# A selective state space recurrence: one state at a time over 128 channels, or 16 states of 8 channels in partitions

## The chip, the cores and the metric

The kernel runs on one core of one Trainium2 chip. The metric is the device time of one execution in microseconds (us). The engines are TensorE (PE in the profile; PEld is its weight load), VectorE (DVE), ScalarE (ACT), GpSimd (POOL) and SyncE (SP, which here only issues DMAs). All arithmetic of the changed part is in fp32.

## The reference

The program is a small two-layer model on x of shape 64 x 32 x 256 (64 sequences of 32 steps). It adds six terms to x one after the other: cross-attention, an RWKV block, a mixture of experts (layer 0), cross-attention with quantised weights, a state space block, a mixture of experts (layer 1). Only the state space block is changed. Cut to what matters, with 512 inner channels d and 16 states n:

```python
xz = x @ in_proj_w.T + in_proj_b
x_main, z = jnp.split(xz, 2, axis=-1)
xc = silu(conv(x_main))                    # 4 taps along the sequence
ssm = xc @ x_proj_w.T + x_proj_b
B_param, C_param = ssm[..., :16], ssm[..., 16:32]
delta = softplus(ssm[..., -1:])            # one step width per token
A = -jnp.exp(A_log)                        # (512, 16)

def step(h, ts):
    dt, B_t, C_t, x_t = ts
    dA = jnp.exp(A[None] * dt[:, :, None])
    dBx = dt[:, :, None] * B_t[:, None, :] * x_t[:, :, None]
    h = dA * h + dBx                       # (batch, 512, 16)
    y = jnp.einsum('bdn,bn->bd', h, C_t) + D * x_t
    return (h, y)

y = scan(step) * silu(z)
out = layernorm(y @ out_proj_w.T + out_proj_b + x)
```

Every pair of channel and state has a recurrence of its own along the sequence, and the output of a channel is a sum over its 16 states.

## The kernel before

The 2048 tokens are cut into four blocks of 512 tokens (`BT` = 512, 16 sequences of 32 steps). Stages 0 to 3 hold layer 0 and the second cross-attention, stage 4 the state space block, stage 5 the experts of layer 1. `layers()` writes down which stage of which block comes when; a scheduler then orders each engine's instructions by that order as a priority and puts the semaphores in. From block 0 on, stage 4 of a block stands ahead of the attention (`s3`) of a later block and the experts (`s5`) of the block before, so that they run side by side. Each engine then works strictly through its own list, and so does the DMA queue of SP.

Stage 4 has three parts. `ahead(b)` normalises x, projects it (L965), convolves it along the sequence and applies silu, which gives `xc` with 128 channels in partitions and 4 groups of channels c; a matmul gives B and C (`ssm`, 32 rows of 512 tokens), which go to DRAM as `rows`; another gives the step width `dt` on all partitions. `gates(v)` computes silu(z) as `zs`. `recur(b, v)` is the recurrence.

In `recur`, POOL first multiplies x by the step (`dtx`, L1036), ACT multiplies x by D (L1041), and then a loop runs over the 16 states n. For a state, its rows of B and C are read from DRAM and spread over all 128 partitions as `bc` (L1045, 512 KB each, on SP). For each of two pairs of channel groups (`c2`), POOL multiplies `dtx` by B into `g` (L1048, 1024 elements for each partition); then for each of the two groups ACT computes exp(A dt) into `h` in PSUM (L1052), DVE runs the scan along the sequence in place (L1053; `dt` of each sequence's first step is set to 1e20, so that nothing carries over), and DVE multiplies by C into `hc` (L1054). POOL adds `hc` to y (L1055). After the loop POOL multiplies y by the gate (L1058), PE projects it (`outps`, L1065), and the layer norm follows. `g`, `hc` and `bc` have two buffers each, `h` has two PSUM banks.

The PSUM banks are held by pools: `ps` (two banks, tag s) serves attention, `psh` (two) the `h` and `outps`, `psp` (one) the projections of `ahead` and `gates`, `psu` (one) the experts' `up`, `psacc` (two) the experts' sums.

Of the kernel before, what the change touches and what calls it, by code (L numbers as in the profile page):

```python
# [8 lines left out]
F32 = mybir.dt.float32  # L9
# [6 lines left out]
P = 128  # L16
# [54 lines left out]
def _chan(k, name, j=0):  # L71
    at = CHAN_AT[name] + j
    return k.chan[:, at : at + 1]
# [844 lines left out]
def _stage4(k, w, wk):  # L918

    nc, i = k.nc, k.i
    N, C = 16, 4
    win = _load_w(k, w, "L1_attn_in_projT", 2, 4 * D)
# [11 lines left out]
    beta = w.tile([P, D], F32, name="beta4", tag="beta4")  # L937
    nc.scalar.dma_start(gamma, i["L1_attn_ln_gamma"].partition_broadcast(P))
    nc.scalar.dma_start(beta, i["L1_attn_ln_beta"].partition_broadcast(P))
    A = w.tile([P, C, N], F32, name="A", tag="A")  # L940
    nc.scalar.dma_start(A, i["L1_attn_A_log"].rearrange("(c p) n -> p c n", p=P))
    nc.scalar.activation(A, A, AF.Exp)

    nc.vector.tensor_scalar(A, A, -1.0, -1e-18, ALU.mult, ALU.min)
# [8 lines left out]
    def ph(shape, name):  # L953
        return k.psh.tile(shape, F32, name=name, tag="h")

    def pp(shape, name):
        return k.psp.tile(shape, F32, name=name, tag="p")

    def tmp(shape, name):
        return wk.tile(shape, F32, name=name, tag="t4", bufs=3)  # L960
# [7 lines left out]
    def ahead(b):  # L968
        v = Ctx()

        xs = [k.x[b][:, j, :] for j in range(4)]
        v.mv, v.rstd = _stats(k, xs, "4")
        x2 = [tmp([P, 2, D], "xn4") for _ in range(2)]
        xn = [x2[j // 2][:, j % 2, :] for j in range(4)]
        for j in range(4):
            _norm(k, xn[j], xs[j], v.mv, v.rstd, j)
        v.xT = wk.tile([P, 2, BT], F32, name="xT4", tag="xT4", bufs=1)
        _to_channels(k, xn, lambda c, ps: nc.scalar.copy(v.xT[:, c, :], ps), pp)

        xc = wk.tile([P, C, 16, T], F32, name="xc", tag="xc")  # L980
        for c in range(C):
            xpad = xpads[c % 2]
            nc.scalar.activation(
                xpad[:, :, 3:], project(v, c, pp).rearrange("p (b t) -> p b t", t=T), AF.Identity, bias=_chan(k, "L1_attn_in_proj_b", c)
            )
# [12 lines left out]
        ssm_ps = pp([2 * N, BT], "ssm_ps")  # L998
        for c in range(C):
            nc.tensor.matmul(ssm_ps, wx[:, c, 0 : 2 * N], v.y[:, c, :], start=c == 0, stop=c == C - 1)  # L1000
        ssm = tmp([2 * N, BT], "ssm")
        nc.scalar.activation(ssm, ssm_ps, AF.Identity, bias=bx)
        v.rows = k.dram.tile([2 * N, BT], F32, name="rows", tag="rows", bufs=2)
        nc.sync.dma_start(v.rows, ssm)

        dt_ps = pp([P, BT], "dt_ps")
        for c in range(C):
            nc.tensor.matmul(dt_ps, wdt[:, c, :], v.y[:, c, :], start=c == 0, stop=c == C - 1)
# [12 lines left out]
        nc.vector.tensor_tensor(l_, l_, e_, ALU.subtract)  # L1021
        nc.vector.scalar_tensor_tensor(dt, dt, 0.0, l_, ALU.max, ALU.add)

        return v

    def gates(v):

        v.zs = wk.tile([P, C, BT], F32, name="zs", tag="zs", bufs=1)
        for c in range(C):
            nc.scalar.activation(v.zs[:, c, :], project(v, C + c, pp), AF.Silu, bias=_chan(k, "L1_attn_in_proj_b", C + c))  # L1030

    def recur(b, v):
        xs = [k.x[b][:, j, :] for j in range(4)]
        dt, y = v.dt, v.y
        dtx = wk.tile([P, C, BT], F32, name="dtx", tag="dtx", bufs=1)
        nc.gpsimd.tensor_tensor(dtx, y, dt.unsqueeze(1).to_broadcast([P, C, BT]), ALU.mult)  # L1036

        nc.gpsimd.memset(dt.rearrange("p (b t) -> p b t", t=T)[:, :, 0:1], 1e20)

        for c in range(C):  # L1040
            nc.scalar.activation(y[:, c, :], y[:, c, :], AF.Copy, scale=_chan(k, "L1_attn_D", c))  # L1041
        bc_rows = v.rows.rearrange("(two n) t -> n two t", two=2)
        for n in range(N):
            bc = wk.tile([P, 2, BT], F32, name="bc", tag="bc", bufs=2)
            nc.sync.dma_start(bc, bc_rows[n].partition_broadcast(P))  # L1045
            for c2 in range(0, C, 2):
                g = wk.tile([P, 2, BT], F32, name="g", tag="g", bufs=2)
                nc.gpsimd.tensor_tensor(g, dtx[:, c2 : c2 + 2], bc[:, 0:1, :].to_broadcast([P, 2, BT]), ALU.mult)  # L1048
                hc = wk.tile([P, 2, BT], F32, name="hc", tag="hc", bufs=2)
                for c in range(2):  # L1050
                    h = ph([P, BT], "h")
                    nc.scalar.activation(h, dt, AF.Exp, scale=A[:, c2 + c, n : n + 1])  # L1052
                    nc.vector.tensor_tensor_scan(h, h, g[:, c, :], 0.0, ALU.mult, ALU.add)  # L1053
                    nc.vector.tensor_tensor(hc[:, c, :], h, bc[:, 1, :], ALU.mult)  # L1054
                nc.gpsimd.tensor_tensor(y[:, c2 : c2 + 2], y[:, c2 : c2 + 2], hc, ALU.add)  # L1055
# [218 lines left out]
def _layouts(inputs):  # L1274
# [22 lines left out]
    for n in ("L1_xattn_ln_gamma", "L1_xattn_ln_beta", "L1_attn_ln_gamma", "L1_attn_ln_beta", "L1_attn_A_log"):  # L1297
        o[n] = a[n]
    for n in ("in_proj", "x_proj", "out_proj"):
        o[f"L1_attn_{n}T"] = a[f"L1_attn_{n}_w"].T  # L1300
    o["L1_attn_x_proj_b"] = a["L1_attn_x_proj_b"][:, None]
# [27 lines left out]
```

## Time and profile before

| | us |
|---|---|
| runs | 2099.62, 2093.59, 2099.14 (median 2099.14) |
| the profiled execution | 2096.84 |
| its span in the profile | 2095.1 |
| first and last start of the scan (L1053) in it | 785.6 and 1909.3 |

The mean granted clock of TensorE over the span is 0.836 of full speed. Times within the span are counted from its start. The profile gives for each engine the busy time and number of instructions; for a group of instructions (line, engine, operation, output and inputs, shapes, count) it gives the busy time, the mean of one in ns, and behind a second bar the idle time of the engine just before them with what ended it. "PE x512" counts matmul records.

| queue | packets | MB | share of the 16 engines |
|---|---|---|---|
| q1 (issued by SP) | 84868 | 147.69 | 23.0% |

### The profile page before, as it was taken

The numbers are of one execution on the slowest core, as the hardware profiler recorded it, in microseconds if no ns is written. First come the engines' busy times: TensorE is split into PE (matmuls) and PEld (weight loads), VectorE is DVE, ScalarE is ACT, GpSimd is POOL, SyncE is SP. The second block draws the span as 40 slices with busy tenths as digits, with TensorE's granted clock in tenths as the row PEclk, the third lists the DMA queues.
The fourth block names the chain that finished last, engine by engine and source line by source line (L and its number), as shares of the span: only waits on it lengthen the run. The fifth ranks groups of instructions, "written<-read, shape, count | busy, mean of one in ns | idle before, by whom it ended". The sixth has DMA issues, their size and how long they took to land. (4 is left out here: it accounts for less than half of the span.)

```text
span 2095.1 us, 20245 instructions
## 1 busy us (share of the span) xinstructions
PE 1644.2 (78%) x6455; PEld 834.1 (40%) x6455; DVE 1391.0 (66%) x2444; ACT 952.6 (45%) x2009; POOL 1013.9 (48%) x1037
## 2 busy tenths in 40 slices
PE   4778966669979788656487798887888987787798
PEld 2334534335545434433234344433444433233343
DVE  5587584775584559889767988655888755876100
ACT  3445342304434174444146566356557445664232
POOL 4445445312121325667625777513767634998000
PEclk8677977889989898558687899888799887999799
DMA  7654232210001011121011232112232112332021
GB/s 239 219 182 144 91 120 80 79 34 21 21 21 43 17 42 51 30 61 61 0 50 53 80 91 90 31 41 65 71 88 73 49 31 66 89 111 77 30 81 40
DMA packets 87540, 149.93 MB, mean 72 GB/s; under 512 B 7672, under 2 KB 51978, under 8 KB 85386
## 3 DMA queue, kind: packets, MB, share of 16 engines
q1 hardware_dynamic: 84868, 147.69, 23.0%
q10 hardware_dynamic: 2566, 0.96, 0.2%
q8 instruction: 51, 0.84, 0.2%
q14 instruction: 55, 0.45, 0.1%
HBM read 137.71 MB, written 10.91 MB: 71 GB/s over the span
## 5 line engine op out<-in xcount | busy, mean ns | idle before, releaser
L1048 POOL TENSOR_TENSOR g<-dtx,bc 128x1024 f32<-128x1024 f32 x128 | 300.4, 2353 | 194.8 <-DVE h L1053 89.4
L1053 DVE TENSOR_TENSOR_SCAN h<-h,g 128x512 f32<-128x512 f32 x256 | 307.3, 1218 | 49.9 <-ACT h L1052 35.1
L1160 PE MATMUL up<-xT,w 128*128 128x512 f32 x512 | 288.1, 678 | 42.5 <-ACT hid L1162 37.3
L1055 POOL TENSOR_TENSOR xc<-xc,hc 128x1024 f32<-128x1024 f32 x128 | 301.0, 2356 | 26.5 <-DVE hc L1054 14.8
L1168 PE MATMUL acc<-hid,w 128*128 128x512 f32 x512 | 250.9, 610 | 15.8 <-ACT hid L1164 15.7
L1052 ACT ACTIVATE h<-dt,A 128x512 f32<-128x512 f32 x256 | 174.0, 692 | 184.5 <-DVE hc L1054 183.3
L1054 DVE TENSOR_TENSOR hc<-h,bc 128x512 f32<-128x512 f32 x256 | 169.7, 679 | 2.9 <-POOL xc L1055 0.5
L1160 PEld LDWEIGHTS up<-xT,w 128*128 128x128 f32 x512 | 97.3, 209 | 165.3 <-issue 79.2
L839 ACT ACTIVATE p<-sc,nm 128x256 f32<-128x256 f32 x256 | 117.6, 471 | 94.5 <-DVE nm L835 83.2
L1162 ACT ACTIVATE hid<-up,chan 128x512 f32<-128x512 f32 x128 | 87.2, 681 | 159.5 <-PE up L1160 159.4
L614 PE MATMUL weps<-we,xT 128*128 128x512 f32 x256 | 139.3, 665 | 17.2 <-DVE x L616 13.9
L1168 PEld LDWEIGHTS acc<-hid,w 128*128 128x128 f32 x512 | 94.1, 194 | 128.2 <-issue 96.3
L828 PE MATMUL sc<-kT,qm 32*128 32x256 f32 x512 | 131.6, 448 | 14.9 <-DVE od L867 11.5
L852 PE MATMUL pt_ps<-ident,p 128*128 128x128 f32 x512 | 97.0, 328 | 53.7 <-ACT p L839 26.6
L833 DVE TENSOR_REDUCE nm<-sc 128x2 f32<-128x512 f32 x128 | 86.3, 686 | 56.2 <-PE sc L828 55.1
L89 POOL TENSOR_TENSOR rs_t<-rs_r 128x4 f32<-128x4 f32 (+3 forms) x138 | 29.7, 218 | 183.1 <-DVE rs_r L87 157.0
L852 PEld LDWEIGHTS pt_ps<-ident,p 128*128 128x128 f32 x512 | 69.5, 165 | 107.1 <-ACT p L839 64.4
L828 PEld LDWEIGHTS sc<-kT,qm 32*128 32x128 f32 x512 | 81.5, 208 | 70.5 <-DVE od L867 20.7
L230 POOL TENSOR_TENSOR cT<-cT,scb 128x2056 f32<-128x2056 f32 x16 | 74.5, 4657 | 53.5 <-DMA scb<-scales 51.8
L1181 DVE SCALAR_TENSOR_TENSOR o<-rT,gt,x 128x256 f32<-128x256 f32 x16 | 7.7, 483 | 139.4 <-PE rT L1180 132.5
L854 ACT COPY pt<-pt_ps 128x512 f32<-128x512 f32 x128 | 74.0, 588 | 40.5 <-PE pt_ps L852 40.3
L514 POOL TENSOR_TENSOR kk<-kk 128x512 f32<-128x512 f32 x32 | 33.1, 1040 | 103.8 <-ACT kk L513 103.8
(389 smaller groups left out, 3218.7 us busy)
## 6 DMA issues: line engine op xcount, KB each, us to landing
bc<-rows SPq DMA_DIRECT2D x64, 512.0 KB
w<-in_L_ffn_w_dram SPq DMA_DIRECT2D x64, 512.0 KB
cT<-in_ctxT_dram SPq DMA_DIRECT2D x16, 1028.0 KB
cq<-cq SPq DMA_DIRECT2D x32, 514.0 KB
cn<-in_ctx_dram SPq DMA_DIRECT2D x64, 256.0 KB
scb<-scales SPq DMA_DIRECT2D x16, 514.0 KB
kb<-steps SPq DMA_DIRECT2D x16, 514.0 KB
x<-in_x_dram SPq DMA_DIRECT2D x4, 512.0 KB
```

Source lines behind the costliest of these rows:

```text
L614: nc.tensor.matmul(ps, xT[:, c, r], we[:, c, e : e + 2, :], start=c == 0, stop=c == 1)
L828: nc.tensor.matmul(sc[h][:, f, :], qm[r, e + f].rearrange("p l n g -> p (l n g)"), kTs[e][r, f, :], start=True, stop=True,)
L839: nc.scalar.activation(w_[:, f, h - h0, :], sc[h][:, f, :], AF.Exp, bias=nm[:, e + f, h : h + 1], accum_out=sm[:, e + f, h : h + 1],)
L852: nc.tensor.transpose(pt_ps[:, h, m, :], ws[e0, hp][:, f, h, m * P : (m + 1) * P], k.ident)
L1048: nc.gpsimd.tensor_tensor(g, dtx[:, c2 : c2 + 2], bc[:, 0:1, :].to_broadcast([P, 2, BT]), ALU.mult)
L1052: nc.scalar.activation(h, dt, AF.Exp, scale=A[:, c2 + c, n : n + 1])
L1053: nc.vector.tensor_tensor_scan(h, h, g[:, c, :], 0.0, ALU.mult, ALU.add)
L1054: nc.vector.tensor_tensor(hc[:, c, :], h, bc[:, 1, :], ALU.mult)
L1055: nc.gpsimd.tensor_tensor(y[:, c2 : c2 + 2], y[:, c2 : c2 + 2], hc, ALU.add)
L1160: nc.tensor.matmul(u, w1[e][:, c, q * P : (q + 1) * P], xT[:, c, :], start=c == 0, stop=c == 1)
L1162: nc.scalar.activation(hid[e][:, q, :], u, AF.Identity, bias=b1)
L1168: nc.tensor.matmul(acc[o], w2[e][:, q, o * P : (o + 1) * P], hid[e][:, q, :], start=n == H, stop=n == E * H + H - 1)
```

## The change

The recurrence is laid out the other way round. A tile of 128 partitions holds 16 states of 8 channels. The 512 channels are 64 such tiles, so the loop still has 64 scans of 128 x 512 for a block.

- `A` is laid out on the host as 16 states times 8 channels in partitions and 64 columns.
- B and C of a block are read from DRAM once, into `bc`, with each state's row spread over its 8 partitions (two DMAs of 256 KB).
- x times the step is computed in `ahead`, per channel group, and written to DRAM as `dtx` (four DMAs of 256 KB). For each pass of the loop two DMAs on SP read 8 channels each from there, spread over the 16 states, into the two halves of `g` (256 KB each); POOL multiplies `g` by B in place.
- The sum over the states is made by TensorE: a matmul with a 0/1 matrix (`red`, a window of 32 columns) adds the 16 states of 8 channels and puts them into their rows of a PSUM bank `y_ps`; 16 matmuls of 128 x 32 by 128 x 512 fill the 128 channels of a group. The sums of a pass are issued after the work of the next pass (`late`). One DVE operation for each group then adds D times x (in place of the multiplication on ACT), and POOL multiplies by the gate.
- POOL's additions of `hc` into y are gone. `g` and `hc` have three buffers in place of two.
- The projections of `ahead` take their PSUM from `ps` (the attention's), those of `gates` from `psu` (the experts'), and `psp` holds `y_ps`.

The diff, cut to its core:

```diff
-    A = w.tile([P, C, N], F32, name="A", tag="A")
-    nc.scalar.dma_start(A, i["L1_attn_A_log"].rearrange("(c p) n -> p c n", p=P))
+    G = 16
+    A = w.tile([P, C * G], F32, name="A", tag="A")
+    nc.scalar.dma_start(A, i["L1_attn_A_log"])
+
+    red = w.tile([P, 56], F32, name="red", tag="red")
+    nc.gpsimd.memset(red, 0.0)
+    nc.vector.tensor_reduce(red[:, 24:32], k.ident.rearrange("p (n d) -> p d n", d=8), AX.X, ALU.add)
...
-    def pp(shape, name):
-        return k.psp.tile(shape, F32, name=name, tag="p")
+    def pa(shape, name):
+        return k.ps.tile(shape, F32, name=name, tag="s")
+
+    def pz(shape, name):
+        return k.psu.tile(shape, F32, name=name, tag="u")
...
-        v.rows = k.dram.tile([2 * N, BT], F32, name="rows", tag="rows", bufs=2)
-        nc.sync.dma_start(v.rows, ssm)
+        rows = k.dram.tile([2, N, BT], F32, name="rows", tag="rows", bufs=2)
+        nc.sync.dma_start(rows.rearrange("w n t -> (w n) t"), ssm)
+        v.bc = wk.tile([P, 2, BT], F32, name="bc", tag="bc")
+        for j in range(2):
+            nc.sync.dma_start(v.bc[:, j], rows[j].unsqueeze(1).to_broadcast([N, 8, BT]))
...
+        v.dtx = k.dram.tile([2 * C, 8 * G // 2, BT], F32, name="dtx", tag="dtx", bufs=2)
+        for c in range(C):
+            dtx = tmp([P, BT], "dtx")
+            nc.gpsimd.tensor_tensor(dtx, v.y[:, c], dt, ALU.mult)
+            nc.sync.dma_start(v.dtx[2 * c : 2 * c + 2].rearrange("h p t -> (h p) t"), dtx)
+
+        nc.gpsimd.memset(dt.rearrange("p (b t) -> p b t", t=T)[:, :, 0:1], 1e20)
...
-        dtx = wk.tile([P, C, BT], F32, name="dtx", tag="dtx", bufs=1)
-        nc.gpsimd.tensor_tensor(dtx, y, dt.unsqueeze(1).to_broadcast([P, C, BT]), ALU.mult)
-
-        nc.gpsimd.memset(dt.rearrange("p (b t) -> p b t", t=T)[:, :, 0:1], 1e20)
-
+
+        dtx = v.dtx.rearrange("h (r q d) t -> h q r d t", r=2, d=8)
+
+        def total(c, q, h2, hc, ps):
+            for r in range(2):
+                m = 32 * (2 * h2 + r)
+                nc.tensor.matmul(
+                    ps[m : m + 32, :], red[:, 24 - 8 * q : 56 - 8 * q], hc[:, r, :], start=q == 0, stop=q == 3, skip_group_check=True,
+                )
+            if q == 3 and h2 == 1:
+                nc.vector.scalar_tensor_tensor(y[:, c, :], y[:, c, :], _chan(k, "L1_attn_D", c), ps, ALU.mult, ALU.add)
+                nc.gpsimd.tensor_tensor(y[:, c, :], y[:, c, :], v.zs[:, c, :], ALU.mult)
+
+        late = []
         for c in range(C):
-            nc.scalar.activation(y[:, c, :], y[:, c, :], AF.Copy, scale=_chan(k, "L1_attn_D", c))
-        bc_rows = v.rows.rearrange("(two n) t -> n two t", two=2)
-        for n in range(N):
-            bc = wk.tile([P, 2, BT], F32, name="bc", tag="bc", bufs=2)
-            nc.sync.dma_start(bc, bc_rows[n].partition_broadcast(P))
-            for c2 in range(0, C, 2):
-                g = wk.tile([P, 2, BT], F32, name="g", tag="g", bufs=2)
-                nc.gpsimd.tensor_tensor(g, dtx[:, c2 : c2 + 2], bc[:, 0:1, :].to_broadcast([P, 2, BT]), ALU.mult)
-                hc = wk.tile([P, 2, BT], F32, name="hc", tag="hc", bufs=2)
-                for c in range(2):
-                    h = ph([P, BT], "h")
-                    nc.scalar.activation(h, dt, AF.Exp, scale=A[:, c2 + c, n : n + 1])
-                    nc.vector.tensor_tensor_scan(h, h, g[:, c, :], 0.0, ALU.mult, ALU.add)
-                    nc.vector.tensor_tensor(hc[:, c, :], h, bc[:, 1, :], ALU.mult)
-                nc.gpsimd.tensor_tensor(y[:, c2 : c2 + 2], y[:, c2 : c2 + 2], hc, ALU.add)
-
-        for c2 in range(0, C, 2):
-            nc.gpsimd.tensor_tensor(y[:, c2 : c2 + 2], y[:, c2 : c2 + 2], v.zs[:, c2 : c2 + 2], ALU.mult)
-        xn = wk.tile([P, 4, D], F32, name="xe4", tag="hc", bufs=2)
+            ps = k.psp.tile([P, BT], F32, name="y_ps", tag="p")
+            for n in range(8):
+                q, h2 = divmod(n, 2)
+                g = wk.tile([P, 2, BT], F32, name="g", tag="g", bufs=3)
+                for r in range(2):
+                    nc.sync.dma_start(g[:, r], dtx[2 * c + h2, q, r].unsqueeze(0).to_broadcast([N, 8, BT]))
+                nc.gpsimd.tensor_tensor(g, g, v.bc[:, 0:1, :].to_broadcast([P, 2, BT]), ALU.mult)
+                hc = wk.tile([P, 2, BT], F32, name="hc", tag="hc", bufs=3)
+                for r in range(2):
+                    h = ph([P, BT], "h")
+                    at = c * G + 4 * (2 * h2 + r) + q
+                    nc.scalar.activation(h, dt, AF.Exp, scale=A[:, at : at + 1])
+                    nc.vector.tensor_tensor_scan(h, h, g[:, r, :], 0.0, ALU.mult, ALU.add)
+                    nc.vector.tensor_tensor(hc[:, r, :], h, v.bc[:, 1, :], ALU.mult)
+                late.append((c, q, h2, hc, ps))
+                if len(late) > 1:
+                    total(*late.pop(0))
+        total(*late.pop(0))
+
+        xn = wk.tile([P, 4, D], F32, name="xe4", tag="hc", bufs=3)
```

More of the change, by code (lines that the diff above doesn't have):

```diff
@@ L977, in ahead @@
         v.xT = wk.tile([P, 2, BT], F32, name="xT4", tag="xT4", bufs=1)
-        _to_channels(k, xn, lambda c, ps: nc.scalar.copy(v.xT[:, c, :], ps), pp)
+        _to_channels(k, xn, lambda c, ps: nc.scalar.copy(v.xT[:, c, :], ps), pa)
         xc = wk.tile([P, C, 16, T], F32, name="xc", tag="xc")
@@ L983, in ahead @@
             nc.scalar.activation(
-                xpad[:, :, 3:], project(v, c, pp).rearrange("p (b t) -> p b t", t=T), AF.Identity, bias=_chan(k, "L1_attn_in_proj_b", c)
+                xpad[:, :, 3:], project(v, c, pa).rearrange("p (b t) -> p b t", t=T), AF.Identity, bias=_chan(k, "L1_attn_in_proj_b", c)
             )
@@ L995, in ahead @@
         v.y = xc.rearrange("p c b t -> p c (b t)")
-        ssm_ps = pp([2 * N, BT], "ssm_ps")
+        ssm_ps = pa([2 * N, BT], "ssm_ps")
         for c in range(C):
@@ L1002, in ahead @@
         nc.scalar.activation(ssm, ssm_ps, AF.Identity, bias=bx)
-        v.rows = k.dram.tile([2 * N, BT], F32, name="rows", tag="rows", bufs=2)
-        nc.sync.dma_start(v.rows, ssm)
-        dt_ps = pp([P, BT], "dt_ps")
+        rows = k.dram.tile([2, N, BT], F32, name="rows", tag="rows", bufs=2)
[3 more added lines that the diff above has]
+            nc.sync.dma_start(v.bc[:, j], rows[j].unsqueeze(1).to_broadcast([N, 8, BT]))
+        dt_ps = pa([P, BT], "dt_ps")
         for c in range(C):
@@ L1029, in gates @@
         for c in range(C):
-            nc.scalar.activation(v.zs[:, c, :], project(v, C + c, pp), AF.Silu, bias=_chan(k, "L1_attn_in_proj_b", C + c))
+            nc.scalar.activation(v.zs[:, c, :], project(v, C + c, pz), AF.Silu, bias=_chan(k, "L1_attn_in_proj_b", C + c))
     def recur(b, v):
@@ L1296, in _layouts @@
     o["L1_xattn_woT"] = a["L1_xattn_wo"].T
-    for n in ("L1_xattn_ln_gamma", "L1_xattn_ln_beta", "L1_attn_ln_gamma", "L1_attn_ln_beta", "L1_attn_A_log"):
+    for n in ("L1_xattn_ln_gamma", "L1_xattn_ln_beta", "L1_attn_ln_gamma", "L1_attn_ln_beta"):
         o[n] = a[n]
+    o["L1_attn_A_log"] = a["L1_attn_A_log"].reshape(64, 8, 16).transpose(2, 1, 0).reshape(P, 64)
     for n in ("in_proj", "x_proj", "out_proj"):
```

## The prediction

> **What bounds the kernel now.** I read the page first (engine shares, costliest groups), then the table of stages, then the waits of the stages in which the recurrence runs, then single instructions.
>
> ```profile
> PE 1644.2 (78%) x6455; PEld 834.1 (40%) x6455; DVE 1391.0 (66%) x2444; ACT 952.6 (45%) x2009; POOL 1013.9 (48%) x1037
> L1048 POOL TENSOR_TENSOR g<-dtx,bc 128x1024 f32<-128x1024 f32 x128 | 300.4, 2353 | 194.8 <-DVE h L1053 89.4
> L1053 DVE TENSOR_TENSOR_SCAN h<-h,g 128x512 f32<-128x512 f32 x256 | 307.3, 1218 | 49.9 <-ACT h L1052 35.1
> L1160 PE MATMUL up<-xT,w 128*128 128x512 f32 x512 | 288.1, 678 | 42.5 <-ACT hid L1162 37.3
> L1055 POOL TENSOR_TENSOR xc<-xc,hc 128x1024 f32<-128x1024 f32 x128 | 301.0, 2356 | 26.5 <-DVE hc L1054 14.8
> L1054 DVE TENSOR_TENSOR hc<-h,bc 128x512 f32<-128x512 f32 x256 | 169.7, 679 | 2.9 <-POOL xc L1055 0.5
> ```
>
> Over the whole span no engine is full, so the shares say little. The groups say what one pass costs. A block has 32 passes (a pass is one g: two scans, two hc products): 2 x 1.218 + 2 x 0.679 = 3.79 us of DVE, and 2.353 + 2.356 = 4.71 us of POOL. Next the stages:
>
> ```profile
> 770.00:1050.00 280.00, 184.83 (x853) 103.57 (x851) 239.79 (x400) 107.87 (x270) 179.67 (x136) 0.68 0.14 40
> 1050.00:1330.00 280.00, 233.27 (x961) 114.63 (x962) 225.91 (x344) 167.25 (x326) 176.23 (x121) 0.86 0.25 74
> 1330.00:1620.00 290.00, 244.91 (x997) 120.87 (x998) 202.46 (x355) 164.57 (x331) 150.95 (x140) 0.86 0.21 59
> 1620.00:1720.00 100.00, 85.08 (x303) 41.50 (x302) 70.41 (x132) 42.23 (x80) 60.21 (x91) 0.85 0.13 43
> 1720.00:1925.00 205.00, 157.04 (x361) 65.74 (x360) 141.99 (x173) 123.55 (x151) 162.53 (x84) 0.93 0.30 85
> ```
>
> The columns are the busy time of PE, PEld, DVE, ACT and POOL, then the clock granted to TensorE, DMA share and GB/s. Block 0's recurrence lies in the first row, 1's in the second, 2's in the third and fourth, 3's in the last. POOL is the fullest engine only in the last row. In the first it is DVE (240 of 280) while PE runs at a clock of 0.68. In the second PE (233) and DVE (226) are both near full; in the third and fourth it is PE, 330 of 390. The scans share these stages with attention (`s3`) and experts (`s5`), which live on PE.
>
> Two more things are to be seen. One is the shortest waits, the other a stretched instruction:
>
> ```profile
> ACT hid L1162 <- PE up L1160: 16.0, 12, 3.4
> DVE h L1053 <- ACT h L1052: 10.3, 9, 3.5
> PE pt_ps L852 <- ACT p L839: 6.1, 6, 2.5
> ```
>
> ```profile
> L835 DVE TENSOR_TENSOR nm<-nm,nsl x64: 146/164/2115, 498.2 to 1645.8; 128x4 f32<-128x4 f32 x64
> L115 DVE TENSOR_SCALAR xe<-x,mv,rstd x16: 401/1856/2553, 1016.8 to 1916.0; 128x256 f32<-128x256 f32 x16
> ```
>
> The first three (total us, times, longest) are waits between 1100 and 1330 us: PE waits for others about 36 us in all there, so it has little slack. The last two give minimum, median and maximum in ns. The operation on 4 elements takes 164 ns, but up to 2115 ns, about as long as one POOL product. At 1784.26 us a small DVE operation (L87) lasts 1.47 us and ends at 1785.73, when POOL's y-addition of 1783.36 + 2.35 ends. So POOL's products hold up certain small DVE operations (not the scan, at most 1232 ns).
>
> **The change, part by part.**
>
> *Removed: POOL's additions into y (L1055).* 32 x 2.356 = 75 us a block. POOL falls from 160 to about 84 us per block (32 products of 2.35, four dtx of 4.51 / 4 = 1.13, four gate products of 1.19). On the path this counts directly only for block 3. It also shortens the stretched DVE operations. From the DVE groups between 770 and 1925 us: L835 46 x (0.707 - 0.161) = 25 us, L115 on x 16 x (1.645 - 0.405) = 20, on xn and xe about 13, L87, L875 and L877 about 18, many small ones about 30: some 105 us. POOL's long products fall to 53%, so I credit 45 us, 11 a block.
>
> *Moved: D times x.* ACT loses 16 x 0.716 us (L1041); DVE gains 16 fused operations on 128x512, nearest row L990 at 0.746 us, so 12 us, 3 a block. Their own cover is the wait for PE; uncovered they cost 12.
>
> *Unchanged:* 256 scans, 256 exponentials, 256 hc products, the two PSUM slots of h. The new layout saves no DVE or ACT work in the loop.
>
> *Added: the sums on PE.* Each pass issues two matmuls, 64 a block. An fp32 matmul is two records (L1160: 256 calls, x512), and the full-clock chain shows 1.72 us for x4, 0.43 a record. A pass so costs at most 1.72 us. Its two matmuls go to different 32-column groups and may overlap: at best 0.86. The nearest row is L862 (128*32, 128 elements, four column groups): x1024 in 74.8 us, 73 ns a record, where 0.43 / 4 at a clock of 0.8 would be 134 ns. Four groups gain 1.8 times; for two I take 1.33 times, 1.29 us a pass, 41 us a block (27 to 55), 48 us at a clock of 0.86.
> The Trainium skill, "TensorEngine Tiling (Array Packing)", Key Properties, speaks against this: changing the tiling mode drains TensorE, and here 128x32 tiles sit between 128x128 ones, so 64 switches a block. This trace shows none where ssm's tiles follow on 128*128 ones (start, us):
>
> ```profile
> 1724.66 1.45 PE L1168 MATMUL acc<-hid,w 128*128 128x512 f32 x3
> 1726.04 3.62 PE L1000 MATMUL ssm_ps<-xc,w_L_attn_x_projT 128*32 128x512 f32 x8
> ...
> 1730.80 3.60 PE L1008 MATMUL dt_ps<-xc,wdt 128*128 128x512 f32 x8
> ```
>
> The switch leaves no gap, and 8 records of either kind take the same time. I go by the row. By the rule, with an estimate of the 0.16 us that a 0.59 us record lasts beyond its 0.43 per switch, it would be 10 us a block more.
> The skill's "TensorE: Matmul & The Clock Gate", Part 1, speaks the other way: a busy PE is granted a faster clock. The trace agrees roughly (0.53 at 28.5 busy us of 50 from 850 us, 1.00 at 45.4 from 1600 us). By it block 0's stage could go from 0.68 to 0.86 and PE's 185 us to 146; by the row alone nothing changes. DVE bounds that stage, so neither moves the sum.
>
> What is queued behind: PE works in order. If an hc is late, the attention and expert matmuls behind its sum wait, and ACT's evictions behind them. One pass of delay (`late`) and three hc buffers cover about 4 us.
>
> *Added: g through DRAM.* Per block 64 loads of 256 KB, 2 of bc and 4 stores of dtx on SP, for 16 loads of 512 KB. At 0.366 us an issue SP spends 26 us a block: hidden. Bytes grow by about 10 MB a block; queue 1 moves 147.69 MB in 23.0% of the span (306 GB/s), so 32 us of all engines a block: hidden at the shares of 0.14 to 0.30. Latency is the danger. A load of 512 KB shows 4.95 to 6.65 us to landing in the chain. A g slot's round is 5.0 (two issues and landing) + 2.35 (product) + 2.44 (two scans) + about 0.9 of handing over = 10.7 us; with three slots one pass per 3.6 us, below DVE's 3.79. Hidden, barely. Without that cover each late microsecond is DVE's. At the start of block 3, store and reload of dtx make about 11.5 us from dt to the first scan; now it is 9.9 (1743.7 to 1753.6). That is +2. In blocks 1 and 2 `ahead` ran a block earlier.
>
> *Moved: PSUM pools.* `ahead` goes to two slots, but beside `s3`; `gates` to the slot of the experts. Between -3 us (its projections now start every 2.7 us for 1.72 us of work) and +3 (a slot still held) a block; I take 0.
>
> *The end of a recurrence:* now two additions and two gate products of 2.35 us follow the last hc; afterwards a sum, 0.75 on DVE and 1.19 on POOL. -5 for block 3; in the others other work lies there.
>
> **Sum.** Block 0 is bound by DVE: -11 + 3, and 3 for sums waited for in order: -5. In the other stages PE becomes the bound. The fullest 50 us beside a recurrence show PE at 46.0 and 45.4 us, so I let PE reach 92%. 1050 to 1330: (233 + 48) / 0.92 = 305, +25. 1330 to 1720: (330 + 48) / 0.92 = 411, +21. 1720 to 1925: (157 + 44) / 0.92 = 219, +14, with +2 and -5: +11. Together +52 on the profiled execution's 2096.8 us, 2149; the median of the runs is 2.3 us above it: 2151 us.
>
> **The rivals.**
> *Faster.* The two sums overlap fully (27 us a block) and PE can be filled to 95% and more, since when it runs late its inputs are ready. Then DVE and POOL decide: -8 a block from the short operations in blocks 0 to 2, and in block 3 DVE's 142 instead of POOL's 162, with -5 at the end. -24 - 20 - 5 = -49: 2050 us. For it: PE's waits of 36 us could shrink. Against it: PE at 83 to 85% already. It decides from a pass under about 0.9 us on PE.
> *Slower still, by the feed.* SP also waits for slots of attention and experts (up to 64.8 us at one wait), and now every pass, not every second one, hangs on it with 10.7 us to fetch. The point is a landing over about 6 us in block 3, where a pass takes 4.2 to 5. If half of the 128 passes lose 1.2 us beyond the 52, it is +75 more: about 2226 us. For it: landings of 6.65 exist. Against it: POOL waits for bc only 21.4 us today.
> *Nothing seen.* PE's growth and the relief of DVE cancel: 2099.
>
> **How the numbers follow.** PE becomes the bound 0.50, with 2115 to 2190; feed 0.25; faster 0.20; cancelled 0.05. The range of 2055 to 2240 leaves out about a tenth at each end. About 0.3% (6 us) is what a measurement of this kernel can tell from no change: faster 0.20, same 0.05, slower 0.75.
>
> **What would show it.** Right: POOL near 715 us busy, PE near 1800, DVE near 1360; PE over 88% in blocks 1 and 2; L835's mean well under 553 ns; the sums' union near 165 us; no large wait of POOL's g for DMA. Wrong: sums near 110 us and PE under 85% in a shorter stage (faster); or g's wait for its load, or PE's wait for hc, at the head of the waits (feed, order).

## The result, and the profile after

| | us |
|---|---|
| changed kernel, 4 runs | 2120.58 to 2137.35, median 2132.90 |
| kernel before, 4 runs on the same chip | 2093.59 to 2105.84, median 2099.38 |
| ratio | 1.0148, 95% interval 1.0101 to 1.0195 |
| profiled execution after | 2137.35, its span 2135.5 (before 2095.1) |

The change makes the kernel 1.5% slower. The page of the changed kernel, its busy times, its chain of work that ended last and its groups (busy us and mean ns behind the first bar, idle before behind the second):

```profile
PE 1805.5 (85%) x6967; PEld 834.8 (39%) x6967; DVE 1324.9 (62%) x2461; ACT 934.8 (44%) x1985; POOL 725.5 (34%) x930
...
PE 50%; DVE 16%; ACT 5%; POOL 4%; issue 4%; DMA 2%; SPq 0%; DVEq 0%; POOLq 0%; ACTq 0%
...
L1075 POOL TENSOR_TENSOR g<-g,bc 128x1024 f32<-128x1024 f32 x128 | 300.8, 2352 | 432.9 <-DMA g<-dtx 340.9
L1081 DVE TENSOR_TENSOR_SCAN h<-h,g 128x512 f32<-128x512 f32 x256 | 307.1, 1220 | 95.2 <-ACT h L1080 43.2
L1189 PE MATMUL up<-xT,w 128*128 128x512 f32 x512 | 274.0, 642 | 12.3 <-ACT hid L1191 12.0
L1060 PE MATMUL y_ps<-hc,red 128*32 128x512 f32 x512 | 246.7, 662 | 38.3 <-DVE hc L1082 37.5
...
L1082 DVE TENSOR_TENSOR hc<-h,bc 128x512 f32<-128x512 f32 x256 | 170.1, 680 | 1.4
```

The chain of the kernel before, for comparison:

```profile
PE 9%; DVE 4%; POOL 4%; ACT 3%; issue 2%; DMA 1%; DVEq 0%; POOLq 0%; SPq 0%; ACTq 0%
```

The shares are of the span, and they add up to 81% now and to 23% before: that is how far back the profile could follow each chain. Of what was followed, PE has 50 of 81 now and had 9 of 23. This is a sign that PE bounds the kernel; the experiments are the test.

PE has gone from 1644 to 1806 us busy, POOL from 1014 to 726, DVE from 1391 to 1325. The scan and the product by C cost what they did before. The new group is L1060, the sums. POOL's wait for its load of `g` is the longest in the page, and it is a trap: POOL has much time to spare now, and in the list of waits DVE waits for POOL's `g` only 21.4 us in all.

The same stages as before, and then the two 50 us in which PE is fullest (busy us of PE, PEld, DVE, ACT, POOL, then granted clock, DMA share, GB/s):

```profile
770.00:1050.00 280.00, 231.25 (x1032) 105.25 (x1031) 227.22 (x431) 104.89 (x277) 111.76 (x118) 0.83 0.28 79
1050.00:1330.00 280.00, 263.90 (x1069) 110.54 (x1068) 205.92 (x347) 156.41 (x312) 100.82 (x88) 0.94 0.37 106
1330.00:1620.00 290.00, 260.36 (x1003) 114.00 (x1003) 178.23 (x332) 152.37 (x301) 98.06 (x117) 0.88 0.32 91
1620.00:1720.00 100.00, 91.24 (x382) 40.18 (x380) 62.40 (x134) 47.28 (x98) 39.34 (x78) 0.93 0.17 48
1720.00:1925.00 205.00, 179.70 (x427) 59.57 (x428) 129.61 (x165) 117.74 (x144) 86.16 (x57) 0.96 0.46 129
1150.00:1200.00 50.00, 48.89 (x194) 18.31 (x193) 39.02 (x59) 30.48 (x61) 20.04 (x10) 0.93 0.44 129
1200.00:1250.00 50.00, 48.95 (x201) 18.61 (x200) 40.48 (x58) 26.68 (x52) 21.35 (x11) 1.00 0.43 125
```

PE is the fullest engine in every row, at 90 to 94% from 1050 to 1720 and at 98% in the last two. The granted clock is higher in every stage than before. DVE and POOL have become emptier everywhere. PE's waits between 1100 and 1330 us have shrunk from 41 us to some 13 (the prediction's 36 left out the shortest ones). The longest now, with total us, times and longest:

```profile
PE y_ps L1060 <- DVE hc L1082: 7.4, 6, 3.7
PE pt_ps L852 <- ACT p L839: 2.3, 2, 1.7
```

The stretched small operations take less time (the first row has busy us and mean ns, the second minimum, median and maximum in ns):

```profile
L835 DVE TENSOR_TENSOR nm<-nm,nsl 128x4 f32<-128x4 f32 x64 | 13.3, 208 | 0.8
L115 DVE TENSOR_SCALAR xe<-x,mv,rstd x16: 323/410/1355, 1002.5 to 1939.5; 128x256 f32<-128x256 f32 x16
```

L835's mean was 553 ns before, so fewer of them are stretched; the longest single one hardly changes (2087 ns for 2115).

From when DVE's scans start and end, the time can be laid out block by block:

| block | scans before, us | scans after, us | end of the block, after minus before | what this block adds |
|---|---|---|---|---|
| 0 | 785.6 to 1014.8 | 782.3 to 1002.6 | -12.2 | -12.2 |
| 1 | 1107.5 to 1321.2 | 1097.1 to 1308.6 | -12.6 | -0.4 |
| 2 | 1444.9 to 1650.4 | 1431.4 to 1668.0 | +17.6 | +30.2 |
| 3 | 1753.6 to 1910.5 | 1771.1 to 1933.6 | +23.1 | +5.5 |
| to the end of the span | 184.6 | 201.9 | +40.4 | +17.3 |

So the change gains in block 0, is even in block 1, and loses in block 2 and behind block 3.

### The profile page after: what moved, and what is told of

Same layout as the page of the kernel before. It is cut to its first block, busy times and chain, and to the rows that moved or that the text cites. A ratio compares the mean times of both kernels' runs of the same rounds, so it can differ in the third digit from the quotient of the medians.

```text
span 2135.5 us, 21568 instructions
## 1 busy us (share of the span) xinstructions
PE 1805.5 (85%) x6967; PEld 834.8 (39%) x6967; DVE 1324.9 (62%) x2461; ACT 934.8 (44%) x1985; POOL 725.5 (34%) x930
## 4 chain that ended last, share of the span: by engine, by line
PE 50%; DVE 16%; ACT 5%; POOL 4%; issue 4%; DMA 2%; SPq 0%; DVEq 0%; POOLq 0%; ACTq 0%
PE up L1189 9%; PE acc L1197 8%; PE y_ps L1060 8%; PE weps L614 4%; PE sc L828 4%; DVE h L1081 3%; PE pt_ps L852 3%; PE oT_ps L862 2%; DVE hc L1082 2%; PE inps L974 1%; PE outps L1094 1%; PE cv L523 1%; DMA g<-dtx 1%; DVE nm L833 1%; DVE xc L999 1%
## 5 line engine op out<-in xcount | busy, mean ns | idle before, releaser
L1075 POOL TENSOR_TENSOR g<-g,bc 128x1024 f32<-128x1024 f32 x128 | 300.8, 2352 | 432.9 <-DMA g<-dtx 340.9
L1189 PE MATMUL up<-xT,w 128*128 128x512 f32 x512 | 274.0, 642 | 12.3 <-ACT hid L1191 12.0
L1060 PE MATMUL y_ps<-hc,red 128*32 128x512 f32 x512 | 246.7, 662 | 38.3 <-DVE hc L1082 37.5
L1197 PE MATMUL acc<-hid,w 128*128 128x512 f32 x512 | 256.6, 618 | 7.8 <-ACT hid L1193 7.8
L1189 PEld LDWEIGHTS up<-xT,w 128*128 128x128 f32 x512 | 91.7, 198 | 156.4 <-issue 115.5
L1197 PEld LDWEIGHTS acc<-hid,w 128*128 128x128 f32 x512 | 93.4, 194 | 134.4 <-issue 113.7
L828 PE MATMUL sc<-kT,qm 32*128 32x256 f32 x512 | 124.7, 429 | 5.8 <-DVE od L867 3.7
L828 PEld LDWEIGHTS sc<-kT,qm 32*128 32x128 f32 x512 | 76.7, 198 | 61.1 <-issue 15.8
L852 PE MATMUL pt_ps<-ident,p 128*128 128x128 f32 x512 | 83.7, 292 | 14.2 <-DVE pp L445 7.9
L852 PEld LDWEIGHTS pt_ps<-ident,p 128*128 128x128 f32 x512 | 61.5, 148 | 72.9 <-ACT p L839 26.1
L1060 PEld LDWEIGHTS y_ps<-hc,red 128*32 128x32 f32 x512 | 32.5, 112 | 134.7 <-DVE hc L1082 79.4
```

The source lines that it names most:

```text
L828: nc.tensor.matmul(sc[h][:, f, :], qm[r, e + f].rearrange("p l n g -> p (l n g)"), kTs[e][r, f, :], start=True, stop=True,)
L852: nc.tensor.transpose(pt_ps[:, h, m, :], ws[e0, hp][:, f, h, m * P : (m + 1) * P], k.ident)
L1060: nc.tensor.matmul(ps[m : m + 32, :], red[:, 24 - 8 * q : 56 - 8 * q], hc[:, r, :], start=q == 0, stop=q == 3, skip_group_check=True,)
L1075: nc.gpsimd.tensor_tensor(g, g, v.bc[:, 0:1, :].to_broadcast([P, 2, BT]), ALU.mult)
L1189: nc.tensor.matmul(u, w1[e][:, c, q * P : (q + 1) * P], xT[:, c, :], start=c == 0, stop=c == 1)
L1197: nc.tensor.matmul(acc[o], w2[e][:, q, o * P : (o + 1) * P], hid[e][:, q, :], start=n == H, stop=n == E * H + H - 1)
```

## Experiments

The theory was that PE has become the bound because the sums take all of what they add, and that what POOL's additions gave back in DVE and POOL pays for a part. The rivals were that the load of each `g` through DRAM (the feed) costs the time, or that the order in PE's queue does. Every ratio is against the kernel before, run beside it on the same chip. Runs on different chips are compared by these ratios; a difference of 0.001 is about 2 us, and the uncertainty of a difference is taken as the root of the two half intervals squared and added.

**The additions of POOL alone, on the kernel before** (e3):

```diff
-                nc.gpsimd.tensor_tensor(y[:, c2 : c2 + 2], y[:, c2 : c2 + 2], hc, ALU.add)
+                if n == N - 1:
+                    nc.gpsimd.tensor_tensor(y[:, c2 : c2 + 2], y[:, c2 : c2 + 2], hc, ALU.add)
```

> The kernel before, with POOL's addition of hc into y left out for all states but the last (so the output lacks 15 of 16 terms). It measures what the removal of those additions alone is worth. If their hold on the small DVE operations and on block 3 is what the change relieves: DVE's busy time falls by 60 to 80 us and the time to 2040 to 2065. If POOL is off the path except in block 3: 2080 to 2090.

Measured: 2044.8 us, ratio 0.9741 [0.9702, 0.9781]. Its page:

```profile
PE 1634.6 (80%) x6455; PEld 832.1 (41%) x6455; DVE 1332.5 (65%) x2444; ACT 952.1 (47%) x2009; POOL 739.0 (36%) x917
```

and its group of the small operation on 4 elements:

```profile
L835 DVE TENSOR_TENSOR nm<-nm,nsl 128x4 f32<-128x4 f32 x64 | 22.0, 343 | 0.8
```

L835's mean falls from 553 to 343 ns, DVE's busy time by 58 us. The additions cost 2.6%, some 54 us. The scans of the four blocks take 209, 196, 190 and 149 us where they took 229, 214, 205 and 157: the relief is spread over all blocks, where the prediction had let POOL's own time count on the path for block 3 alone.

**Is that relief POOL's occupancy, or what its reads do to DVE?** (e8) The additions are replaced by memsets of about the same length.

```diff
-                nc.gpsimd.tensor_tensor(y[:, c2 : c2 + 2], y[:, c2 : c2 + 2], hc, ALU.add)
+                if n == N - 1:
+                    nc.gpsimd.tensor_tensor(y[:, c2 : c2 + 2], y[:, c2 : c2 + 2], hc, ALU.add)
+                else:
+                    nc.gpsimd.memset(hc, 0.0)
+                    nc.gpsimd.memset(hc, 0.0)
+                    nc.gpsimd.memset(hc[:, 0, 0:400], 0.0)
```

> The kernel before, with POOL's addition of hc into y replaced in 15 of 16 states by three memsets of hc (1024, 1024 and 400 elements, about 2.3 us together by the rate of 0.95 us for 1056 elements; the output lacks these terms). POOL stays as busy, waits for the same hc and releases it as late, but reads nothing. If the additions cost by holding up small DVE operations through SBUF reads: these shrink and the time is near the 2045 of the kernel without the additions, 2045 to 2065. If POOL's own time and the late release of hc cost: 2085 to 2100.

Measured: 2071.56 us, ratio 0.9903 [0.9871, 0.9935], between the two expectations. Its groups (one of the memsets, and L835):

```profile
L1059 POOL MEMSET hc<- 128x1024 f32 x120 | 114.4, 953 | 5.4
L835 DVE TENSOR_TENSOR nm<-nm,nsl 128x4 f32<-128x4 f32 x64 | 27.0, 422 | 0.8
```

POOL is as busy as before (1005 us) and DVE at 1353 us lies between the 1391 before and the 1333 of e3. Of the 2.6%, 1.0% comes without freeing POOL; the other 1.6% [1.1, 2.1] needs POOL's time and its later release of `hc`. The split is rough. L835's mean of 422 ns is not the memsets' doing: the ten that start inside a memset take 153 ns on average, and all 13 of over 300 ns end together with one of POOL's products (11 with `g`, 2 with `dtx`). But three L87 that start inside a memset take 0.91 to 1.00 us, where those that start with POOL idle take 0.17 on average, so a memset is not free for all of DVE's small operations.

**The sums in bf16** (e1): `hc` and the ones are written in bf16, so that a sum is one record and not two. `hc` is thereby rounded before it is summed; nothing else changes.

```diff
-    red = w.tile([P, 56], F32, name="red", tag="red")
+    red = w.tile([P, 56], BF16, name="red", tag="red")
...
-                hc = wk.tile([P, 2, BT], F32, name="hc", tag="hc", bufs=3)
+                hc = wk.tile([P, 2, BT], BF16, name="hc", tag="hc", bufs=3)
```

> The changed kernel with hc and the 0/1 matrix in bf16, so that a sum is one pass of TensorE in place of the two of fp32. If the sums on PE are what costs (247 us busy in the changed kernel), they fall to about 65 us, PE as a whole to 1650 or less, and what remains of the change is its relief of POOL and DVE: 2050 to 2080 us, faster than the kernel before. If the load of g through DRAM or the order of SP's queue costs the time, PE falls in the same way and the time stays within 10 us of 2133.

Measured: 2082.03 us, ratio 0.9926 [0.9895, 0.9958]. Page and group of the sums:

```profile
PE 1697.6 (82%) x6711; PEld 838.6 (40%) x6711; DVE 1318.1 (63%) x2462; ACT 938.3 (45%) x1987; POOL 723.8 (35%) x930
...
L1062 PE MATMUL y_ps<-hc,red 128*32 128x512 bf16 x256 | 99.9, 435 | 41.7 <-DVE hc L1084 38.1 <-DVE xc L1066 3.1
```

With half of the records the sums take 100 us instead of 247, PE falls by 108, and the time falls by 2.2% (47 us, give or take 12): below the kernel before. That is the first expectation in kind, but less than it said: it had the sums at 65 us, PE at 1650 or less and the time at 2080 at most. The product that writes `hc` takes 678 ns in bf16 and 680 in fp32, so this is PE's doing. PE still waits 38 us for `hc` ahead of the sums, as in the changed kernel: waiting in order for `hc` is not what differs.

**Four column groups in a row** (e2): both `h2` halves are summed together in the program, and the pass of delay is gone.

```diff
-            for r in range(2):
-                m = 32 * (2 * h2 + r)
+            for j in range(4):
                 nc.tensor.matmul(
-                    ps[m : m + 32, :], red[:, 24 - 8 * q : 56 - 8 * q], hc[:, r, :], start=q == 0, stop=q == 3, skip_group_check=True,
+                    ps[32 * j : 32 * j + 32, :], red[:, 24 - 8 * q : 56 - 8 * q], hcs[j // 2][:, j % 2, :], start=q == 0, stop=q == 3, skip_group_check=True,
```

> The changed kernel with the sums of two passes issued together, so that four matmuls for the four column groups follow each other (fp32 as before; one pass of delay less, three hc buffers). In the changed kernel the records of a pass's two groups follow each other every 0.43 us, without any overlap, against my 1.33 times. If four groups in a row overlap as in attention (L862, about 1.8 times), the sums' busy time falls from 247 to about 140 us and the time to 2085 to 2110. If groups don't overlap at 512 columns, it stays near 247 us and the time is 2133 to 2155, the more so as hc is held longer.

Measured: 2136.01 us, ratio 1.0174 [1.0136, 1.0212]; the group of the sums:

```profile
L1059 PE MATMUL y_ps<-hc,red 128*32 128x512 f32 x512 | 252.9, 660 | 34.3 <-DVE hc L1081 33.8
```

Nothing is gained: 253 us for the same 512 records. But the traces bear out neither the edit's aim, four sums in a row, nor the expectation's premise, that the two groups never overlap. Two rows of the changed kernel (start, length, what ran), in which x4 are the records of the two sums of a pass:

```profile
1818.78 1.05 PE L1060 MATMUL y_ps<-hc,red 128*32 128x512 f32 x4
1819.76 0.70 PE L1189 MATMUL up<-xT,w 128*128 128x512 f32 x1
```

And rows of e2, in which x2 are the records of a single sum:

```profile
1824.52 1.05 PE L1059 MATMUL y_ps<-hc,red 128*32 128x512 f32 x2
1825.50 1.12 PE L1188 MATMUL up<-xT,w 128*128 128x512 f32 x2
...
1829.45 1.05 PE L1059 MATMUL y_ps<-hc,red 128*32 128x512 f32 x4
```

Two sums in two column groups take 1.05 us, as long as one sum alone; at 1818.78 their first records start 7 ns apart. So two groups of 512 columns do run side by side when nothing stands between them in PE's order. Mostly something does: the scheduler has put other matmuls between the two sums in 98 of the changed kernel's 128 passes, and among the four sums in 63 of e2's 64. So e2 does not test four groups in a row, and whether four would overlap stays open.

One row of the changed kernel looks like four records of 0.43 us one after the other with a tail:

```profile
1812.54 1.92 PE L1060 MATMUL y_ps<-hc,red 128*32 128x512 f32 x4
```

It is two pairs at half the clock: the granted clock from 1812.50 to 1814.40 us is 0.50, and from 1818.70 to 1819.80 it is 1.00.

**The feed, taken away** (e4): `g` is made from a tile already in SBUF, and the 256 loads are gone.

```diff
-                for r in range(2):
-                    nc.sync.dma_start(g[:, r], dtx[2 * c + h2, q, r].unsqueeze(0).to_broadcast([N, 8, BT]))
-                nc.gpsimd.tensor_tensor(g, g, v.bc[:, 0:1, :].to_broadcast([P, 2, BT]), ALU.mult)
+                nc.gpsimd.tensor_tensor(g, v.zs[:, 0:2, :], v.bc[:, 0:1, :].to_broadcast([P, 2, BT]), ALU.mult)
```

> The changed kernel without the loads of g: POOL makes g from zs in SBUF times B (so the output is not that of the recurrence; the stores of dtx stay, sums and scans too). If PE's sums bound the changed kernel: within 12 us of 2133. If the feed through DRAM costs the time: 2100 or less.

Measured: 2132.01 us, ratio 1.0156 [1.0114, 1.0198]; the group of the sums:

```profile
L1060 PE MATMUL y_ps<-hc,red 128*32 128x512 f32 x512 | 257.8, 653 | 36.7 <-DVE hc L1080 32.6 <-DVE xc L1064 3.6
```

The same time as with the loads (1.0148), and the same load on PE (1807 us). POOL's 341 us of waiting for DMA have gone and bought nothing: the feed is hidden, by PE.

**A quarter of the sums** (e5): only the last `q` is summed, in fp32.

```diff
-            for r in range(2):
+            for r in range(2 if q == 3 else 0):
...
-                    ps[m : m + 32, :], red[:, 24 - 8 * q : 56 - 8 * q], hc[:, r, :], start=q == 0, stop=q == 3, skip_group_check=True,
+                    ps[m : m + 32, :], red[:, 24 - 8 * q : 56 - 8 * q], hc[:, r, :], start=True, stop=True, skip_group_check=True,
```

> The changed kernel with only every fourth sum (q = 3 alone, still fp32; the output lacks three quarters of the terms). The new layout, the loads of g and the pools of PSUM stay. If PE's sums are all that the change costs, the sums take about 62 us of PE and the time lands a little above that of the kernel before with one addition (2045): 2050 to 2070 us. If the rest of the change (feed, pools, start of a block) costs something of its own: 2080 or more.

Measured: 2082.75 us, ratio 0.9941 [0.9919, 0.9964].

```profile
L1060 PE MATMUL y_ps<-hc,red 128*32 128x512 f32 x128 | 60.6, 661 | 21.2 <-DVE hc L1082 21.2
```

That is the second expectation: the rest of the change costs something of its own. With 39 us less of sums than in e1 there is no less time, so time is not linear in PE's load, as the first expectation had it. Something holds both at about 2082. The run also shows that fp32 in `hc` itself is not the cost: DVE writes it in fp32 here, and the time is that of e1.

**The feed taken away where PE has room** (e6 is e1 with the edit of e4):

> The changed kernel with bf16 sums and without the loads of g (g from zs in SBUF, so the output is not that of the recurrence). With fp32 sums the loads cost nothing, as PE was the bound. If PE is still the bound with bf16 sums: 2075 to 2090, as with the loads (2082). If the loads are next in line behind PE: 2065 or less.

Measured: 2046.83 us, ratio 0.9784 [0.9756, 0.9812]. Its group of the product:

```profile
L1075 POOL TENSOR_TENSOR g<-zs,bc 128x1024 f32<-128x1024 f32 x128 | 301.6, 2359 | 398.9 <-DVE h L1081 298.6 <-ACT zs L1051 24.1 <-DVE nm L835 20.8
```

POOL now waits for DVE to release a slot, as a producer with spare time should. Here the feed is worth 1.4% (30 us, give or take 9). This is what holds e1 at 2082.

**The floor from the other side** (e7 is e1 with every sum issued twice):

```diff
-                nc.tensor.matmul(
-                    ps[m : m + 32, :], red[:, 24 - 8 * q : 56 - 8 * q], hc[:, r, :], start=q == 0, stop=q == 3, skip_group_check=True,
-                )
+                for n2 in range(2):
+                    nc.tensor.matmul(
+                        ps[m : m + 32, :], red[:, 24 - 8 * q : 56 - 8 * q], hc[:, r, :], start=q == 0 and n2 == 0, stop=q == 3 and n2 == 1, skip_group_check=True,
+                    )
```

> The changed kernel with bf16 sums, each of them issued twice (so that the recurrence's part of y is doubled). PE gets its 512 records back, of half the length: about 200 us busy in place of 100. If PE's time is what counts, whatever the type: 51 us for 147 us of sums between fp32 and bf16 makes about 35 us for 100: 2110 to 2125. If it was something else about fp32 hc (its writes on DVE, its loads into PE): 2082 to 2092.

Measured: 2088.33 us, ratio 0.9961 [0.9938, 0.9984].

```profile
L1063 PE MATMUL y_ps<-hc,red 128*32 128x512 bf16 x512 | 154.6, 427 | 53.5 <-DVE hc L1085 50.1 <-DVE xc L1067 2.9
```

55 us more of sums move the time by 0.35%, give or take 0.39. The time lies in the range that was to speak for something else about fp32, but e5 has ruled out the writes of `hc`, and the sums came to 155 us, not 200. With PE at 1670 (e5), 1698 (e1) and 1726 us (e7) the floor holds; with 1806 it is exceeded by 47. So PE takes over somewhere between 1726 and 1806 us, if only its load counts; no run here has bf16 sums at the load of the fp32 ones.

**A fourth buffer for `g`** (e9 is e1 with this; the space comes from `hc`, and the tile `xe4` that shared its buffers gets one of its own):

```diff
-                g = wk.tile([P, 2, BT], F32, name="g", tag="g", bufs=3)
+                g = wk.tile([P, 2, BT], F32, name="g", tag="g", bufs=4)
...
-                hc = wk.tile([P, 2, BT], F32, name="hc", tag="hc", bufs=3)
+                hc = wk.tile([P, 2, BT], BF16, name="hc", tag="hc", bufs=2)
...
-        xn = wk.tile([P, 4, D], F32, name="xe4", tag="hc", bufs=3)
+        xn = wk.tile([P, 4, D], F32, name="xe4", tag="xe4", bufs=1)
```

> The changed kernel with bf16 sums, g with four buffers in place of three, and hc with two in place of three (SBUF is full; hc in bf16 needs half). The loads of g cost 35 us here (2082 with them, 2047 without). If it is the round of three slots (10.7 us for a pass of about 4), a fourth takes most of it away: 2050 to 2065. If it is the order of SP's queue, where g's loads and the experts' weights wait for each other, or the start of a block: 2075 to 2090.

Measured: 2067.0 us, ratio 0.9876 [0.9828, 0.9924], the fastest of those that leave nothing out. From its waits:

```profile
POOL g L1077 <- DMA g<-dtx: 270.9, 79, 8.1
```

In e1 this wait was 329.4 us with a longest of 12.2. The time lies between the two expectations, and the step from e1, 0.5% give or take 0.6, is not separated from none by these runs.

**The loads on another queue** (e10 is e1, e11 is e9, each with this):

```diff
-                    nc.sync.dma_start(g[:, r], dtx[2 * c + h2, q, r].unsqueeze(0).to_broadcast([N, 8, BT]))
+                    nc.scalar.dma_start(g[:, r], dtx[2 * c + h2, q, r].unsqueeze(0).to_broadcast([N, 8, BT]))
```

> The changed kernel with bf16 sums and the loads of g issued from ACT's queue in place of SP's (three buffers as before). ACT pays about 64 x 0.37 = 24 us a block of issue, of which it has room (45% busy). If the cost of the loads is the order of SP's queue: 2055 to 2070. If it is the round of the three slots: 2075 to 2095, or more if ACT waits for g's slots ahead of its exponentials.

> Both: four buffers of g and its loads on ACT's queue. If slots and queue order each carry a part: about 2050, the 2047 of the kernel without the loads. If ACT's issue and waits cost as much as SP's order did: as with four buffers alone.

Measured: 2171.21 us, ratio 1.0375 [1.0327, 1.0422], and 2197.47, ratio 1.0504 [1.0453, 1.0554]. Two large misses. ACT's timeline in e10 shows one piece of it (in brackets, the idle time before and what ended it):

```profile
1834.42 1.17 ACTq L1076 DMA_DIRECT2D g<-dtx  x2
1835.62 1.28 ACT L1051 ACT_TABLE_LOAD   x1 [2.36 <-DVE h L1083]
```

A load has to wait until a scan has read its slot, and on ACT whatever stands behind the load waits with it: 2.36 us here, of which 1.17 are the two issues, and the next instruction is a gate that has nothing to do with `g`. The 256 issues, at 0.52 us each, take some 134 us of ACT. PE has the same matmuls as in e1 and is busy 1742 us for 1698, at a mean clock of 0.820 for 0.852, so a part of the loss passes through PE. That all this together makes 4.5% is argued, not shown.

**One load a pass** (e12 is e9 with `dtx` laid out in DRAM such that one load of 512 KB fetches a whole `g`, at the price of 16 stores of 64 KB a block for 4 of 256):

```diff
-                for r in range(2):
-                    nc.sync.dma_start(g[:, r], dtx[2 * c + h2, q, r].unsqueeze(0).to_broadcast([N, 8, BT]))
+                nc.sync.dma_start(g.rearrange("p r t -> p (r t)"), dtx[2 * c + h2, q].unsqueeze(0).to_broadcast([N, 8, 2 * BT]))
```

> bf16 sums, four buffers of g, two of hc, loads on SP, and dtx laid out in DRAM so that both halves of a pass lie together: one load of 512 KB a pass (4 KB for each partition) in place of two of 256 KB, for 16 stores of 64 KB a block in place of four of 256 KB. A pass saves one issue (0.37 us or more) and half of its packets. If the loads' latency and issue are what is left of their cost (2067 with four buffers, 2047 without loads): 2050 to 2062. If only bytes or the waits for SP's other loads are left: 2062 to 2072.

Measured: 2084.4 us, ratio 0.9951 [0.9928, 0.9973], and the wait of the product:

```profile
POOL g L1077 <- DMA g<-dtx: 354.3, 84, 13.9
```

By the ratios it is 0.75% slower than e9, give or take 0.53, and slower than either expectation. Half the issues, and the wait for them is longer than e9's 270.9. So fewer issues alone do not make the feed faster. As the stores changed too, the run does not separate issuing from the rest; what makes the feed slow (the size of one transfer, the small stores, where in the queue they stand) stays open.

## Why the prediction was right, and where it was not

**The mechanism held.** Forecast 2151 us and slower; measured 2132.9. PE becomes the bound: it is busy 92% of the time from 1050 to 1720 us, a cut in its load is worth 2.2% (e1), and the loads of `g` cost nothing while it is the bound (e4). Without feed the fp32 records are worth 3.7%, 78 us (e4 against e6).

**How the parts add up.** The prices depend on the order. One path of single steps: POOL's additions gone -54 us (e3); layout, PSUM pools and sums in bf16 without the feed +9, not separated from none (e6 against e3); the feed +30 (e1 against e6); fp32 +47 (changed kernel against e1). That these come to the measured +31 is no evidence, since each step starts where the last one ended. The other path takes fp32 first, +78, and then the feed, nothing (e4). Feed and fp32 hide each other, as if the larger of the two decided, so neither has one price. The move of the PSUM pools, which I took at 0, was not tested by itself.

**Sums: too small, by the order on PE.** A pass took 1.93 us (246.7 us for 128 passes) for the predicted 1.29, more than the 1.72 that I had called the most. I let the two sums of a pass follow each other on PE. Where they do, two take 1.05 us at full clock, less than I had (the row at 1818.78); apart, each takes that long, and in 98 of 128 passes other matmuls stand between them. No run here keeps them together. At 1.05 us a pass they would take 134 us, an estimate at full clock.

**The change of tiling mode: not free.** I read the lines from 1724.66 us on as showing no gap. But from 1724.66 to 1726.04 three records take 1.38 us, 0.09 more than 3 x 0.43. In the changed kernel's trace, at full clock, the record behind one of 512 columns starts 429 ns after it where both are on 128x128 tiles (891 of 892 within one line), and 523 ns after it where the tile changes to 128x32 or back (95 of 96 and 146 of 149). The Trainium skill says that changing the tiling mode drains TensorE ("TensorEngine Tiling (Array Packing)", Key Properties); this trace agrees, with about 0.09 us a switch, and a sum that stands alone among 128x128 tiles pays it twice.

**PE's other work: the clock rule was dismissed, and should not have been.** PE came out at 1806 where I said near 1800, but by luck: two errors cancel. Counted in the trace, all matmuls but the sums cover 1596 us, 48 less than the 1644 before, and the sums add 209 us to that (247, of which 38 overlap other matmuls), 44 more than the 165 predicted. The mean granted clock rose from 0.836 to 0.878, and in the five stages from 0.68, 0.86, 0.86, 0.85 and 0.93 to 0.83, 0.94, 0.88, 0.93 and 0.96. Over the runs it rises with PE's share of the span: 78% and 0.836 before, 82% and 0.852 in e1, 85% and 0.878 here (roughly: e10 has 80% and 0.820). That agrees with the rule of "TensorE: Matmul & The Clock Gate", Part 1, in the Trainium skill, that a busy PE is granted a faster clock. I wrote that it moves nothing because DVE bounds block 0, and didn't apply it to the stages where PE is the bound: from 1050 to 1330 us, 233 us at 0.86 would be 213 at 0.94, by this estimate 20 of the 25 us that I charged there.

**PE filled to 92%: right for the stages.** From 1050 to 1720 us PE was busy 615.5 of 670 us, which is 92%. Single stretches of 50 us held 48.9, or 98%: once PE runs late its inputs are ready, as the rival "faster" had said. What that rival needed beside it, a pass under 0.9 us on PE, was missing.

**Where the loss lies.** For block 1's stage I said +25 and it added nothing. Block 0 gained 12 for 5. Blocks 2 and 3 with what follows lost 53 us (30 + 5.5 + 17) where I said +32. By the estimate above the first error is mostly the clock. The last expert matmul of block 2 (L1168, now L1197) ends 54 us after the last scan instead of 33, so a part of the loss comes out as a longer tail.

**Relief of DVE: too small.** I credited 45 us of 105. DVE's busy time fell 66 us, and 78 before the 12 for the fused product by D; e3 alone shows 58. I also let it count only where DVE bounds; e3 shows 54 us over all blocks, and e8 that 1.6 [1.1, 2.1] of its 2.6% hang on POOL's time, which I had counted on the path for block 3 alone.

**Feed: hidden, but not for the reason given.** I took 0.366 us for an issue, from the row of `bc`; the loads of `g` took 0.572. That makes a slot's round 11.1 us and a pass 3.7, still under DVE's 3.79. By this the loads should have kept up with DVE. They were hidden (e4), but by PE: 30 us appear as soon as PE has room (e6). "No large wait of POOL's g for DMA" was wrong too (340.9 us). By my own list this wait at the head of the waits spoke for the rival "feed"; e4 shows that it costs nothing here, so it was the wrong sign to name.

## What to carry to other kernels

Before you move work to an engine that is 80 to 85% full, let that engine have both what it gets from a busier clock and what it gets from inputs that are ready, and count on two matmuls running side by side only where nothing stands between them in the engine's order: look there before you call a cost the hardware's. Two costs beside each other have no price each: take one away with the other present and absent (here e4 against e6), or the first experiment will call a cost nothing that is only covered. The additions on POOL were worth taking away; the matmul that replaced them, with its sums apart in PE's order, paid only in bf16. With a fourth buffer that version, 2067 us at 0.9876 of the time before, is the fastest here that leaves nothing out, though not separated from three buffers. fp32 sums kept together were not tried.

## What the runs showed of the hardware that was not expected

- Two fp32 sums of 512 columns in different column groups take 1.05 us together, as long as one alone (x4 at 1818.78 in the changed kernel, x2 at 1824.52 in e2). Other matmuls between them undo this.
- A switch between 128x128 and 128x32 tiles costs PE about 0.09 us (523 ns from start to start in place of 429).
- With 209 us of matmuls added, the others covered 1596 us in place of 1644, at a mean clock of 0.878 for 0.836.
- A 4-element DVE operation (L835, with two inputs) that starts inside a POOL memset takes 153 ns (e8, ten of them); all 13 that were stretched there end together with a POOL product, which reads. Another small one (L87) is held up by a memset too, 0.91 to 1.00 us for 0.17.
- The same loads cost 4.5% more time on ACT's queue than on SP's (e10 against e1).
